# Attention over all tokens: the products with the values in a budget per turn, and none of them in a block's extra turn

## The chip, the core and the metric

One NeuronCore of a Trainium2 chip runs the whole kernel in one launch. TensorE (PE in the profile) multiplies matrices, ScalarE (ACT) evaluates functions, VectorE (DVE) adds and divides, GpSimd (POOL) does some adds and issues DMAs, SyncE (SP) issues DMAs. The metric is the device time of one execution in microseconds (us), the median of three runs. Lower is better.

## The reference, cut to what matters

The model is a chain of four layers on 4 images of 56 x 56 positions with 128 channels. The first layer attends within windows, and then over all 3136 positions of an image; the second part is what the change touches. Everything is float32.

```python
def _mha(x, wq, bq, wk, bk, wv, bv, wo, bo):
    n, s, c = x.shape                      # s = 3136, c = 128, NH = 4 heads, dk = 32
    q = (x @ wq + bq).reshape(n, s, NH, dk).transpose(0, 2, 1, 3)
    ...
    scores = jnp.einsum('nhqd,nhkd->nhqk', q, k) / jnp.sqrt(jnp.float32(dk))
    attn = jax.nn.softmax(scores, axis=-1)
    out = jnp.einsum('nhqk,nhkd->nhqd', attn, v)
    out = out.transpose(0, 2, 1, 3).reshape(n, s, c)
    return out @ wo + bo
...
xf = x.reshape(B, H * W, C)
xf = xf + _mha(_layernorm(xf, g1, be1), wq, bq, wk, bk, wv, bv, wo, bo)
h = jax.nn.gelu(_layernorm(xf, g2, be2) @ w1 + b1, approximate=False)
xf = xf + (h @ w2 + b2)
```

After this layer come a graph layer over pairs of positions in a row, a Fourier layer with its own attention over rows, and a convolution. They are not changed.

## The kernel before, in words

The kernel works through the four images one after the other: `fast_attention` (which first calls `fast_windows` for the attention in windows and for the queries, keys and values), then the multilayer perceptron, then the graph layer. When all four are done, the Fourier layer, its attention and the last convolution follow. Each of these stages needs the result of the one before, so the attention loop of an image stands on the way to everything after it.

`fast_attention` cuts the 3136 queries of an image into 7 blocks of 448 (`NBLK`, `NB`). For each block it goes through the keys in 24 chunks of 128 and a remainder of 64, which it counts as chunk 24. A chunk of a block has four tiles, one for each head: 128 keys by 448 queries of scores. So a block has 96 tiles and an image 672. They are counted through, over the ends of blocks.

The loop takes 7 tiles per *turn* (`TURN`), so an image has 96 turns. A turn has two halves, of four tiles and of three:

- PE multiplies the queries and keys (L698) into a PSUM tile, `s0` of four banks for the first half and `s1` of three for the second. Each has one buffer.
- ACT takes the exponential of all tiles of the half in one instruction (L701) and writes it into a ring in SBUF of 28 tiles (`RING`), which is 7 chunks or four turns. A tile's slot is its number modulo 28.
- For every chunk that is now complete, `add` issues the sum over the keys, which is the denominator of the softmax: DVE adds the chunk to a running sum (L626, L630); chunks 1, 5, 9, 13 and 17 (`BY_DMA`) are instead copied (SP, L618) or added (POOL, L620) into a second sum by DMA, which DVE adds in (L629) ahead of the block's last chunk. In the last block chunks 21 to 23 are left to a product with ones on PE.

Then `values` issues the products of the exponentials with the values (L642). A chunk is four products of 32 columns each, one per head, side by side in the array, summed in one PSUM bank (`f_po`). The lists `queue` and `ready` give them a lag of one turn: a turn's `values` takes all chunks in `ready`, up to the end of a block, and then moves the chunks that this turn completed from `queue` to `ready`. As 7 tiles are 1.75 chunks, the turns have 2, 2, 2 and 1 chunks in rotation. When chunk 23 is through, ACT copies the block's sum out of the bank (L645).

Two turns after a block's tiles began to be complete for the block before (`AFTER`, `ends`), an *extra turn* follows the ordinary one. It has three parts:

- `remainder(j)`: the scores of the 64 last keys of the block j that has begun (L660, into `s0`), and their exponential (L663, tile `f_p`);
- `values` once more, with whatever is ready;
- `finish(j - 1)`: the denominators of the block before, as products with ones: of DVE's sum (L671) and of the remainder (L674), into `s1`; then the output product of the block before that one (L677); a copy by ACT (L679), the reciprocal (L680) and the product (L681) by DVE, and the addition to the residual (L686).

The order of PE, ACT and DVE in this loop is the order of the program: it is written out by hand (`manual_schedule`), and each engine works through its own list in that order. PE writes into `s0` or `s1` only when ACT has read what was in it, and ACT writes into a slot of the ring only when PE, DVE or the DMA have read it.

One float32 matmul stands in the trace as two, its two passes through the array. So a first half of scores is x8 in the timeline, a whole turn of scores x14, and a chunk of values x8. The matmul columns read rows * columns of the array, then the shape that streams.

Of the kernel before, what the change touches and what calls it, by code (L numbers as in the profile page):

```python
# [23 lines left out]
NB = 448  # L24
# [16 lines left out]
def blk(j):  # L41
    return slice(j * NB, (j + 1) * NB)
# [524 lines left out]

RING = 28
TURN = 7
BY_DMA = (1, 5, 9, 13, 17)  # L570
BY_ONES = ()
LAST_ONES = (21, 22, 23)
# [3 lines left out]
def fast_attention(k, w, xw, xf, beside, mr):  # L576

    nc, tc = k.nc, k.tc
    scale = 1.0 / math.sqrt(32.0)
    heads = [slice(32 * h, 32 * h + 32) for h in range(4)]
    half = (slice(0, 64), slice(64, 128))
    with ExitStack() as es:
        big = es.enter_context(tc.tile_pool(name="f_big", bufs=1))
        qT = big.tile([P, TOK], F32, name="f_qT")
        kT = big.tile([P, TOK], F32, name="f_kT")
        va = big.tile([P, 25, P], F32, name="f_va")  # L590
        fast_windows(k, w, xw, xf, mr, beside, qT, kT, va)

        ring = es.enter_context(tc.tile_pool(name="f_ring", bufs=1)).tile([P, RING, NB], F32, name="f_ring")
        wk = es.enter_context(tc.tile_pool(name="f_wk", bufs=2))
        ps = es.enter_context(tc.tile_pool(name="f_ps", bufs=1, space=PSUM))
        oT = es.enter_context(tc.tile_pool(name="f_out", bufs=1)).tile([P, TOK], F32, name="f_oT")
        blocks = [Env() for _ in range(NBLK)]
        queue, ready = [], []

        def by_ones(j):  # L600
            return LAST_ONES if j == NBLK - 1 else BY_ONES

        def bank(turn):
            return ps.tile([P, (4, 3)[turn], 512], F32, tag="s%d" % turn, name="f_s%d" % turn)

        def slots(j, c):
            s = (96 * j + 4 * c) % RING
            return ring[:, s:s + 4, :]

        def add(j, c):  # L610

            e = blocks[j]
            if c in by_ones(j):
                return
            if c in BY_DMA:
                if c == BY_DMA[0]:
                    e.far = wk.tile([P, 4, NB], F32, name="f_far", bufs=1)
                    nc.sync.dma_start(e.far, slots(j, c))  # L618
                else:
                    nc.gpsimd.dma_start(e.far, slots(j, c), accum_op=ALU.add)  # L620
                return
            if c == 0:
                return
            if not hasattr(e, "acc"):
                e.acc = wk.tile([P, 4, NB], F32, name="f_acc")
                nc.vector.tensor_add(e.acc, slots(j, 0), slots(j, c))  # L626
                return
            if BY_DMA and c == last_add(j):
                nc.vector.tensor_add(e.acc, e.acc, e.far)  # L629
            nc.vector.tensor_add(e.acc, e.acc, slots(j, c))  # L630

        def last_add(j):
            return max(c for c in range(24) if c not in BY_DMA and c not in by_ones(j))

        def value(j, c):
            e = blocks[j]
            if c == 0:
                e.po = ps.tile([P, 512], F32, tag="po", name="f_po")
            for h in range(4):
                o = half[h % 2] if c == 24 else slice(0, P)  # L640
                p = e.p24[o, h // 2, :] if c == 24 else slots(j, c)[:, h, :]
                nc.tensor.matmul(e.po[heads[h], :NB], va[o, c, heads[h]], p, start=(c == 0), stop=(c == 23))  # L642
            if c == 23:
                e.raw = wk.tile([P, NB], F32, name="f_raw")
                nc.scalar.copy(e.raw, e.po[:, :NB])  # L645

        def values():

            while ready:
                j, c = ready.pop(0)  # L650
                value(j, c)
                if c == 23:
                    break
            ready.extend(queue)
            queue.clear()

        def remainder(j):
            ss = bank(0)
            for h in range(4):
                nc.tensor.matmul(ss[half[h % 2], h // 2, :NB], kT[heads[h], 24 * P:TOK], qT[heads[h], blk(j)],  # L660
                                 start=True, stop=True)
            blocks[j].p24 = wk.tile([P, 2, NB], F32, name="f_p24")
            nc.scalar.activation(blocks[j].p24, ss[:, 0:2, :NB], AF.Exp, scale=scale)  # L663

        def finish(j):

            e = blocks[j]
            pd = bank(1)
            for n, p in enumerate([e.acc] + [slots(j, c) for c in by_ones(j)]):
                for h in range(4):  # L670
                    nc.tensor.matmul(pd[heads[h], 0, :NB], k.ones[:, 0:32], p[:, h, :], start=(n == 0), stop=False)  # L671
            for h in range(4):
                o = half[h % 2]
                nc.tensor.matmul(pd[heads[h], 0, :NB], k.ones[o, 0:32], e.p24[o, h // 2, :], start=False, stop=True)  # L674
            m = 1 + (j > 0)
            if j:
                nc.tensor.matmul(pd[:, 1, :NB], w.wo, oT[:, blk(j - 1)], start=True, stop=True)  # L677
            den = wk.tile([P, 2, NB], F32, name="f_den")
            nc.scalar.copy(den[:, :m], pd[:, :m, :NB])  # L679
            nc.vector.reciprocal(den[:, 0], den[:, 0])  # L680
            nc.vector.tensor_mul(oT[:, blk(j)], e.raw, den[:, 0])  # L681
            if j:
                output(j - 1, den[:, 1])

        def output(j, pm):
            nc.vector.scalar_tensor_tensor(xf[:, blk(j)], pm, w.fbvo, xf[:, blk(j)], ALU.add, ALU.add)  # L686

        with tc.manual_schedule(engines={mybir.EngineType.PE, mybir.EngineType.Activation, mybir.EngineType.DVE}):
            t = 0
            ends = {-(-96 * j // TURN) - 1 + AFTER: j for j in range(NBLK)}  # L690
            for turn in range(96 * NBLK // TURN):
                for half_turn in range(2):
                    m = (4, 3)[half_turn]
                    ss = bank(half_turn)
                    for i in range(m):
                        j, c = divmod((t + i) // 4, 24)
                        h = (t + i) % 4
                        nc.tensor.matmul(ss[:, i, :NB], kT[heads[h], c * P:(c + 1) * P], qT[heads[h], blk(j)],  # L698
                                         start=True, stop=True)
                    slot = t % RING  # L700
                    nc.scalar.activation(ring[:, slot:slot + m, :], ss[:, :m, :NB], AF.Exp, scale=scale)  # L701
                    for q in range(t // 4, (t + m) // 4):
                        queue.append(divmod(q, 24))
                        add(*divmod(q, 24))
                    t += m
                values()
                if turn in ends:
                    j = ends[turn]
                    remainder(j)
                    values()  # L710
                    if j:
                        finish(j - 1)
                    queue.append((j, 24))
            while ready or queue:
                values()
            finish(NBLK - 1)
        pm = ps.tile([P, 512], F32, tag="po", name="f_pf")
        nc.tensor.matmul(pm[:, :NB], w.wo, oT[:, blk(NBLK - 1)], start=True, stop=True)
        output(NBLK - 1, pm[:, :NB])
# [1750 lines left out]
def build(k, packs, I, out):  # L2470
# [3 lines left out]
    with ExitStack() as es:  # L2474
# [15 lines left out]
        with tc.tile_pool(name="w01", bufs=1) as wp, tc.tile_pool(name="io", bufs=1) as io:  # L2490
# [47 lines left out]
            with tc.If(small_scores > 0) as small:  # L2538
                for b in range(B):
                    first_layers(lambda *a: fast_attention(*a, functools.partial(norms, b - 1), k.mr[:, b, :]), I["x"][b],  # L2540
                                 x2d[b] if b < B - 1 else None, loaded=b == 0)
# [78 lines left out]
```

## Time and profile before

| | us |
|---|---|
| median of 3 runs | 3779.57 |
| lowest and highest | 3778.22, 3781.8 |
| the profiled execution, its own time | 3777.02 |
| the profiled execution, its span | 3775.2 |
| busy in the span: PE, DVE, ACT, POOL | 3456.1, 2762.1, 2069.6, 1305.6 |
| the four attention loops in the trace | 151.6 to 515.0, 847.5 to 1210.2, 1544.0 to 1906.7, 2239.7 to 2606.7 |

The span is from the first instruction to the last on the core; 1.8 us of the profiled execution's time lie around it. In a line of groups stand the line, engine, operation, output and inputs, shapes and count, then the busy time in us and the mean of one in ns, then the idle time before these instructions and what ended it. In a timeline stand the start and length in us of instructions of one kind that follow each other, and in brackets the idle time before them and what ended it. The length of a matmul includes its way through the array, which lies beside the next one, so the cost of a group in a stream is read from start to start. Some matmul records can be missing, so a count in the timeline may be short.

### The profile page before, as it was taken

The numbers are of one execution on the slowest core, as the hardware profiler recorded it, in microseconds if no ns is written. First come the engines' busy times: TensorE is split into PE (matmuls) and PEld (weight loads), VectorE is DVE, ScalarE is ACT, GpSimd is POOL, SyncE is SP. The second block draws the span as 40 slices with busy tenths as digits, with TensorE's granted clock in tenths as the row PEclk, the third lists the DMA queues.
The fourth block names the chain that finished last, engine by engine and source line by source line (L and its number), as shares of the span: only waits on it lengthen the run. The fifth ranks groups of instructions, "written<-read, shape, count | busy, mean of one in ns | idle before, by whom it ended". The sixth has DMA issues, their size and how long they took to land. (4 is left out here: it accounts for less than half of the span.)

```text
span 3775.2 us, 78990 instructions
## 1 busy us (share of the span) xinstructions
PE 3456.1 (92%) x35064; PEld 1544.1 (41%) x35064; DVE 2762.1 (73%) x2635; ACT 2069.6 (55%) x2052; POOL 1305.6 (35%) x779
## 2 busy tenths in 40 slices
PE   6899999989999998899989989999997889998998
PEld 4422234552223455322244542223456433335664
DVE  6488877857887786688869748887785767775676
ACT  4587865448777554687745448876553001213452
POOL 0000016600000471000018400000663769993676
PEclk8999999999999998999999999999998999999999
DMA  2134310004333000244310013443002047862011
GB/s 98 39 87 91 89 40 19 20 18 98 86 90 70 19 3 19 76 89 97 88 30 3 19 37 89 98 89 83 2 9 86 2 84 154 171 139 86 30 40 52
DMA packets 93656, 239.56 MB, mean 63 GB/s; under 512 B 64380, under 2 KB 66172, under 8 KB 88060
## 3 DMA queue, kind: packets, MB, share of 16 engines
q0 software_dynamic: 16128, 102.77, 13.6%
q1 hardware_dynamic: 18492, 118.82, 9.9%
q10 hardware_dynamic: 58688, 12.85, 2.0%
q8 instruction: 277, 4.54, 0.5%
q14 instruction: 71, 0.58, 0.1%
HBM read 79.46 MB, written 26.51 MB: 28 GB/s over the span
## 5 line engine op out<-in xcount | busy, mean ns | idle before, releaser
L701 ACT ACTIVATE f_ring<-f_s 128x1792 f32<-128x1792 f32 (+1 forms) x768 | 1091.5, 1477 | 186.1 <-PE f_s L698 125.4
L630 DVE TENSOR_TENSOR f_acc<-f_acc,f_ring 128x1792 f32<-128x1792 f32 x464 | 939.5, 2025 | 174.0 <-ACT f_ring L701 142.1
L698 PE MATMUL f_s<-f_qT,f_kT 32*128 32x448 f32 x5376 | 723.0, 573 | 66.3 <-ACT f_ring L701 42.5
L620 POOL DMA_DIRECT2D f_far<-f_ring x112 | 96.4, 861 | 1693.5 <-ACT f_ring L701 1441.7
L642 PE MATMUL f_po<-f_ring,f_va 128*32 128x448 f32 x5376 | 584.8, 546 | 0.0
L1063 DVE TENSOR_TENSOR e_td<-e_pa,e_c 128x1792 f32<-128x1792 f32 x252 | 491.2, 2012 | 14.4 <-ACT e_a L1028 14.4
L1065 POOL TENSOR_TENSOR e_tp<-e_a,e_c 128x1792 f32<-128x1792 f32 x140 | 451.9, 3258 | 143.8 <-PE e_acc L1070 104.8
L698 PEld LDWEIGHTS f_s<-f_qT,f_kT 32*128 32x128 f32 x5376 | 256.7, 183 | 537.5 <-ACT f_ring L701 410.7
L1070 PE MATMUL e_acc<-e_td,t_shared 32*32 32x448 f32 x8064 | 322.9, 545 | 21.8 <-DVE e_td L1063 10.6
L1067 ACT ACTIVATE e_tp<-e_tp 128x1792 f32<-128x1792 f32 x140 | 235.1, 1697 | 174.3 <-POOL e_tp L1065 174.3
L1679 DVE TENSOR_TENSOR u_ud<-u_px,u_d 112x1792 f32<-112x1792 f32 x144 | 240.1, 1707 | 94.8 <-PE u_po L1684 85.7
L642 PEld LDWEIGHTS f_po<-f_ring,f_va 128*32 128x32 f32 x5376 | 135.8, 109 | 396.3 <-issue 383.3
L1070 PE MATMUL e_acc<-e_tp,t_shared 32*32 32x448 f32 x4480 | 221.2, 544 | 3.2 <-ACT e_tp L1067 2.5
L1684 PE MATMUL u_po<-u_ud,AT 112*64 112x448 f32 x960 | 200.7, 548 | 23.3 <-DVE u_ud L1679 23.3
L1681 POOL TENSOR_TENSOR u_up<-xh,u_d 112x1792 f32<-112x1792 f32 x64 | 193.8, 3054 | 24.0 <-PE u_po L1684 12.4
L1070 PEld LDWEIGHTS e_acc<-e_td,t_shared 32*32 32x32 f32 x8064 | 133.3, 103 | 147.1 <-DVE e_td L1063 55.8
L680 DVE RECIPROCAL f_den<-f_den 128x448 f32<-128x448 f32 x28 | 82.7, 2953 | 94.7 <-ACT f_den L679 94.7
L1546 POOL TENSOR_TENSOR q_u<-iS,q_g 128x1792 f32<-128x1792 f32 x32 | 102.8, 3236 | 72.1 <-PE s_px L1394 48.0
L1684 PE MATMUL u_po<-u_up,AT 112*64 112x448 f32 x576 | 125.1, 541 | 0.9 <-POOL u_up L1681 0.8
L1684 PEld LDWEIGHTS u_po<-u_ud,AT 112*64 112x64 f32 x960 | 64.8, 137 | 147.6 <-issue 86.6
L1070 PEld LDWEIGHTS e_acc<-e_tp,t_shared 32*32 32x32 f32 x4480 | 94.5, 103 | 55.6 <-ACT e_tp L1067 19.1
L891 ACT ACTIVATE m_hT<-m_ph,w_fb 128x392 f32<-128x392 f32 x128 | 72.7, 588 | 70.4 <-PE m_ph L890 64.9
(487 smaller groups left out, 4746.0 us busy)
## 6 DMA issues: line engine op xcount, KB each, us to landing
f_far<-f_ring POOLq DMA_DIRECT2D x112, 896.0 KB, 6.4
u_d<-dd SPq DMA_DIRECT2D x48, 784.0 KB
f_far<-f_ring SPq DMA_DIRECT2D x28, 896.0 KB
xw<-in_x SPq DMA_DIRECT2D x4, 1568.0 KB
x2d<-x SPq DMA_DIRECT2D x4, 1568.0 KB
xad<-x SPq DMA_DIRECT2D x4, 1568.0 KB
x_xs<-xad ACTq DMA_DIRECT2D x32, 196.0 KB
xm<-x_ev ACTq DMA_DIRECT2D x64, 98.0 KB
```

The lines of the kernel that those rows point to most:

```text
L630: nc.vector.tensor_add(e.acc, e.acc, slots(j, c))
L642: nc.tensor.matmul(e.po[heads[h], :NB], va[o, c, heads[h]], p, start=(c == 0), stop=(c == 23))
L698: nc.tensor.matmul(ss[:, i, :NB], kT[heads[h], c * P:(c + 1) * P], qT[heads[h], blk(j)], start=True, stop=True)
L701: nc.scalar.activation(ring[:, slot:slot + m, :], ss[:, :m, :NB], AF.Exp, scale=scale)
L1063: nc.vector.tensor_tensor(t, am, cm, ALU.max)
L1065: nc.gpsimd.tensor_sub(t, bc(a.rearrange("p (l n) -> p l n", l=8), 1, 4), cm)
L1067: nc.scalar.activation(tf, tf, AF.Relu)
L1070: nc.tensor.matmul(acc[quarters[q], r, :NB], k.ident[o, o], t[o, q].rearrange("p l n -> p (l n)"), start=(g == 0), stop=(g == len(EDGE_TUR ...
L1546: nc.gpsimd.tensor_mul(u, bc(st.iS[:, bp, c, :HH], 1, HEADS), bc(g[:, n, c, :], 2, HH))
L1679: nc.vector.tensor_mul(u, bc(px[:, :, :NB], 2, m), dm)
L1681: nc.gpsimd.tensor_mul(u, bc(x, 2, m), dm)
L1684: nc.tensor.matmul(po[64 * b2:64 * b2 + 64, :NB], st.AT[:, 8 * i + h0 + q, 2 * bp + b2, :], u[:, b2, q, :], start=(left == 16), stop=(left ...
```

## The change

Four things are changed in `fast_attention`:

- A chunk's products with the values can be split into two halves of 224 queries. An entry of `ready` now has a part: the whole (`WHOLE`) or one half.
- `values` takes a budget of half chunks, `ROOM`: 3, 3, 4 and 4 in turns 0, 1, 2 and 3 of every four, and one more where more than three entries are waiting. Where one half of room is left, it does half of a chunk and leaves the other half first in the list. It still ends at chunk 23. What is left stays in `ready`.
- In the extra turn there is no `values`. The remainder's own product with the values (chunk 24) is done at the end of `finish` if the block has begun its products, and is else put into the list. Before, it was queued.
- In `finish` the output product of the earlier block stands ahead of the product of ones with the remainder, and not behind it.

After the last turn the list is emptied with a budget of 4 a call. In the order of issue an image has 52 halves, two for each of 26 split chunks. The lists of DVE, POOL and SP keep their order; in ACT's, four of the seven copies of L645 stand one turn later.

```diff
+ROOM = (3, 3, 4, 4)
+WHOLE = slice(0, NB)
...
-        def value(j, c):
+        def value(j, c, part):
             e = blocks[j]
-            if c == 0:
+            if c == 0 and part.start == 0:
                 e.po = ps.tile([P, 512], F32, tag="po", name="f_po")
             for h in range(4):
                 o = half[h % 2] if c == 24 else slice(0, P)
-                p = e.p24[o, h // 2, :] if c == 24 else slots(j, c)[:, h, :]
-                nc.tensor.matmul(e.po[heads[h], :NB], va[o, c, heads[h]], p, start=(c == 0), stop=(c == 23))
-            if c == 23:
+                p = e.p24[o, h // 2, part] if c == 24 else slots(j, c)[:, h, part]
+                nc.tensor.matmul(e.po[heads[h], part], va[o, c, heads[h]], p, start=(c == 0), stop=(c == 23 and part.stop == NB))
+            if c == 23 and part.stop == NB:
                 e.raw = wk.tile([P, NB], F32, name="f_raw")
                 nc.scalar.copy(e.raw, e.po[:, :NB])
-
-        def values():
-
-            while ready:
-                j, c = ready.pop(0)
-                value(j, c)
-                if c == 23:
+                return True
+
+        def values(room):
+
+            while ready and room > 0:
+                j, c, part = ready.pop(0)
+                if room == 1 and part == WHOLE:
+                    part = slice(0, NB // 2)
+                    ready.insert(0, (j, c, slice(NB // 2, NB)))
+                room -= 2 if part == WHOLE else 1
+                if value(j, c, part):
                     break
-            ready.extend(queue)
-            queue.clear()
...
-        def finish(j):
+        def finish(j, left=None):
...
+            m = 1 + (j > 0)
+            if j:
+                nc.tensor.matmul(pd[:, 1, :NB], w.wo, oT[:, blk(j - 1)], start=True, stop=True)
             for h in range(4):
                 o = half[h % 2]
                 nc.tensor.matmul(pd[heads[h], 0, :NB], k.ones[o, 0:32], e.p24[o, h // 2, :], start=False, stop=True)
-            m = 1 + (j > 0)
-            if j:
-                nc.tensor.matmul(pd[:, 1, :NB], w.wo, oT[:, blk(j - 1)], start=True, stop=True)
+            if left is not None:
+                value(left, 24, WHOLE)
...
-                        queue.append(divmod(q, 24))
+                        queue.append((*divmod(q, 24), WHOLE))
                         add(*divmod(q, 24))
                     t += m
-                values()
+                values(ROOM[turn % 4] + (len(ready) > 3))
+                ready.extend(queue)
+                queue.clear()
                 if turn in ends:
                     j = ends[turn]
                     remainder(j)
-                    values()
-                    if j:
-                        finish(j - 1)
-                    queue.append((j, 24))
-            while ready or queue:
-                values()
+                    if not j:
+                        ready.append((0, 24, WHOLE))
+                    else:
+                        started = hasattr(blocks[j], "po")
+                        finish(j - 1, j if started else None)
+                        if not started:
+                            ready.append((j, 24, WHOLE))
+            while ready:
+                values(4)
             finish(NBLK - 1)
```

## The prediction

> **What bounds the kernel now.** I read the share of the engines first, then the costliest groups of the page, then the timeline inside the loop that the diff edits. The groups:
>
> ```profile
> L701 ACT ACTIVATE f_ring<-f_s 128x1792 f32<-128x1792 f32 (+1 forms) x768 | 1091.5, 1477 | 186.1 <-PE f_s L698 125.4
> L630 DVE TENSOR_TENSOR f_acc<-f_acc,f_ring 128x1792 f32<-128x1792 f32 x464 | 939.5, 2025 | 174.0 <-ACT f_ring L701 142.1
> L698 PE MATMUL f_s<-f_qT,f_kT 32*128 32x448 f32 x5376 | 723.0, 573 | 66.3 <-ACT f_ring L701 42.5
> L642 PE MATMUL f_po<-f_ring,f_va 128*32 128x448 f32 x5376 | 584.8, 546 | 0.0
> ```
>
> Scores (L698), exponentials (L701), sums (L630) and value products (L642) are the four dearest groups of the edited code. They lie in one loop, run once for each of 4 samples. Busy time of the engines in the first sample's loop, from its first score to the end of its last denominators:
>
> ```profile
> 151.60:515.00 363.40, 347.36 (x2948) 106.31 (x2948) 286.98 (x147) 289.65 (x215) 24.22 (x28) 1.00 0.40 90
> ```
>
> Columns after the length: PE, PE loads, DVE, ACT, POOL, clock. PE is the fullest (347 of 363 us), but a busy PE counts the tails of matmuls, so the waits have to be found in the timeline. Four ordinary turns of the loop:
>
> ```profile
> 226.52 1.78 PE L698 MATMUL f_s<-f_qT,f_kT 32*128 32x448 f32 x14
> 228.23 1.71 PE L642 MATMUL f_po<-f_ring,f_va 128*32 128x448 f32 x16
> 229.87 1.78 PE L698 MATMUL f_s<-f_qT,f_kT 32*128 32x448 f32 x14
> 231.58 0.96 PE L642 MATMUL f_po<-f_ring,f_va 128*32 128x448 f32 x8
> 232.69 1.03 PE L698 MATMUL f_s<-f_qT,f_kT 32*128 32x448 f32 x8
> 233.87 1.03 PE L698 MATMUL f_s<-f_qT,f_kT 32*128 32x448 f32 x6
> 234.83 1.71 PE L642 MATMUL f_po<-f_ring,f_va 128*32 128x448 f32 x16
> 236.47 1.78 PE L698 MATMUL f_s<-f_qT,f_kT 32*128 32x448 f32 x14
> ```
>
> and ACT in the same turns:
>
> ```profile
> 227.62 2.85 ACT L701 ACTIVATE f_ring<-f_s 128x1792 f32<-128x1792 f32 x2 [0.51 <-PE f_s L698]
> 230.97 5.66 ACT L701 ACTIVATE f_ring<-f_s 128x1792 f32<-128x1792 f32 x4 [0.51 <-PE f_s L698]
> 237.57 2.85 ACT L701 ACTIVATE f_ring<-f_s 128x1792 f32<-128x1792 f32 x2 [0.94 <-PE f_s L698]
> ```
>
> Starts give the prices. The seven scores of a turn take 228.23 - 226.52 = 1.71 us. Two chunks of values (x16: 2 chunks, 4 heads, two passes each) take 229.87 - 228.23 = 1.64. One chunk alone, where nothing waits, takes 0.89 (322.65 to 323.54 below is such a one), so a chunk is 0.75 and a change of the array's tiling about 0.14. A turn with two chunks is 3.35 us and PE sets it; ACT works 2.85 and idles 0.5. A turn with one chunk would be 1.71 + 0.89 = 2.60, less than ACT's 2.85. Then ACT sets it: the two turns from 229.87 to 236.47 take 6.60 against 2.60 + 3.35 = 5.95 of PE work, and PE has lost 0.65. Nothing gives it back, for PE sets the next turns. A block's extra turn, to the second turn after it:
>
> ```profile
> 312.56 0.98 PE L660 MATMUL f_s<-f_qT,f_kT 32*64 32x448 f32 x8
> 313.47 1.71 PE L642 MATMUL f_po<-f_ring,f_va 128*32 128x448 f32 x16
> 315.00 0.94 PE L671 MATMUL f_s<-f_acc,c_ones 128*32 128x448 f32 x8
> 315.86 0.96 PE L674 MATMUL f_s<-f_p,c_ones 64*32 64x448 f32 x8
> 316.75 1.02 PE L677 MATMUL f_s<-f_oT,t_first 128*128 128x448 f32 x2
> 317.70 2.09 PE L698 MATMUL f_s<-f_qT,f_kT 32*128 32x448 f32 x14
> 320.51 2.21 PE L698 MATMUL f_s<-f_qT,f_kT 32*128 32x448 f32 x14 [0.72 <-ACT f_ring L701]
> 322.65 0.96 PE L642 MATMUL f_po<-f_p,f_va 64*32 64x448 f32 x8
> 323.54 0.96 PE L642 MATMUL f_po<-f_ring,f_va 128*32 128x448 f32 x8
> ```
>
> The extra turn takes two chunks that PE has no need to do there; ACT, which gets no scores, stands still. Then the turn at 317.70 has no values at all: 2.81 us to 320.51 for 1.71 of work, and the next takes 3.92 (to 324.43) for 3.48. PE loses 1.10 + 0.44 = 1.54.
>
> **What the Trainium skill says.** "TensorE: Matmul & The Clock Gate", section "Step-by-step: what each phase is for", has weights of later matmuls loaded while earlier ones run; the trace agrees (a group of four loads takes 0.13 us inside a pass of 0.37). Its section "Wait — 56ns, not 53.3ns?" gives a floor of about 25 ns from start to start for a small matmul, so four of a half pass would need 0.10 us; an estimate, and the trace's own row below is used instead. "TensorEngine Tiling (Array Packing)", section "Key Properties", says that a change of tiling mode drains TensorE; that is the 0.14 above, and halves do not change the mode.
>
> **The change, part by part.** PE's own work in one sample's loop before: 96 turns x 1.71 = 164.2; 175 chunks (168 and 7 remainders) x 0.747 = 130.7; 96 groups of values x 0.15 for the switch back and its gap = 14.4; 7 remainders x (0.91 + 0.14) = 7.4; 7 finishes x (0.87 + 0.87) + 6 output products x 0.95 + three more chunks of ones in the last block x 0.75 = 20.1. Sum 336.8. The loop takes 363.4, so PE waits 26.6. The order of issue has 22 turns with one chunk and 6 with none after the extra turns: 22 x 0.65 + 6 x 1.54 = 23.5, and the rest is the start (ACT's table load). So the waits are explained, and they are what the change can win.
>
> *Budget of 3 and 4 half chunks.* Seven chunks per four turns as before, so nothing is left over. A turn of three halves costs 1.71 + 3 x 0.373 + 0.15 + 0.02 = 3.00, one of four 3.35. ACT's second exponential of a turn ends 1.10 + 2.85 = 3.95 after the turn's start; the next turn's second group of scores needs its bank and could start at 3.00 + 0.75 = 3.75, so it waits until about 4.02: 0.27 lost. After the second turn of three halves ACT ends at 6.8, and the second group comes at 7.0: no wait. So four turns take 2 x 3.00 + 2 x 3.35 + 0.27 = 12.97, where they took 239.82 - 226.52 = 13.30. At most 24 such pairs stand in a sample, about 20 undisturbed by block ends: 20 x 0.27 = 5.4 of waits remain.
>
> *A half is a new operation*: 224 columns, 52 of them in a sample. Streaming at this trace's rate (448 columns per 0.373 us pass) it takes 0.187 a pass. Nearest row: the score products of the windows (L381, 196 columns, two tiles beside each other), 16 in 1.38 us, 0.172 per pair against 0.163 at that rate: 0.01 over. I take 0.02 per half (two passes): 1.0 us per sample. Lower bound 0, as columns must stream. Upper bound: the loads do not hide, 0.13 per pass, 0.26 per half, 13.5 us, of which the 0.27 wait of the pairs would swallow some 5.4: net 8 us less gain per sample.
>
> *No chunk in the extra turn.* The two chunks move to the two turns behind it, which then have 3 or 4 halves and wait as ordinary turns do. The 1.54 goes; what comes is a wait in the finish: it starts 0.91 after L660 and needs the bank of the second exponential, which ends 3.95 after the turn before began. Behind a four-half turn (3.35 + 0.91) it waits for nothing, behind a three-half one or one that stops at chunk 23 for 0.1 to 0.9. I take 0.5 for each of 6: 3.0. DVE's last sum before it ended at 309.38, 361.05 and 411.66 for blocks that start the extra turn at 312.56, 361.08 and 412.84, so the new start, 0.91 after L660, has 0.94 us to spare in the tightest and 4.1 in the widest. In two of the six the chunk of the remainder lands behind the ones (PE 0.75, ACT's copy runs beside it); in four the block has not begun and it is queued: the same work. Moving the output product ahead of the remainder's ones changes no work and covers the remainder's exponential (0.91 + 0.87 + 0.95 = 2.7 us against 1.05 + 0.92).
>
> *The ring.* Chunks now lag by up to five in the queue. An exponential overwrites a slot four turns later; in the order of issue every chunk read from such a slot stands before that turn's scores, so PE gives no new wait. The order of DVE's and POOL's instructions is unchanged: a loop that is 14 us shorter leaves DVE 287 busy of 350, and chunks for the accumulating DMA come every 7.4 instead of 7.6 us, with 0.86 to issue and 6.4 to land: 7.3, just under. *The end*: three chunks instead of two stay for the drain, contained in the work.
>
> Sum for one sample: work 336.8 + 1.0 + 0.2 (one more group) = 338.0; waits 5.4 + 3.0 + 3.1 for the start = 11.5; together 349.5 to 349.8, against 363.4: 13.8 less. Four samples run alike (loops of 363.4, 362.7, 362.7 and 367.0 us) and what follows each waits for it: 4 x 13.8 = 55 us. The profiled execution took 3777.0 (span 3775.2), which would be 3722; the median is 2.6 above it, so 3724.5.
>
> **Rivals.** *Dear halves*: loads or issue bind a half pass. For it: no row has this shape. Against: L381, and 66-column matmuls (L396) at 0.065 a pair. With 0.26 per half the gain is 13.8 + 1.0 - 8 = some 6.5 per sample: 3754. *Nothing gained*: a half pass costs a whole one, 52 x 0.373 = 19.4 a sample less what the pairs swallow: within 6 us of 3779. *Slower*: DVE is late at the block's end. Place: L671 now starts 1.5 us sooner after L660, on the path of PE and of the copy on ACT behind it. It decides once the last sum ends over 0.9 us after L660 begins; each us beyond costs 24 us in the kernel (6 blocks, 4 samples). With some 2.3 us to spare on the mean of the three blocks above, sums that end 6 us later against L660 than now lose 3.7 a block: 24 x 3.7 = 89, less 55: 3813. For it: DVE would be 287 of 350 busy, and one block is tight. Against: DVE still waits for L701 142 us in all ahead of its sums, so it is not behind.
>
> **Chances.** Forecast 0.78 (3714 to 3738: 2 us per sample for the waits that I took by hand, and halves at 0 to 0.07); dear halves 0.13 (to 3754); nothing gained 0.04; slower 0.05. The range takes in the dear halves: 3714 to 3754. About 0.2% (7.6 us) is what a measurement of this kernel tells from no change: faster 0.90, same 0.05, slower 0.05.
>
> **What would show it.** Turns of 3.0 and 3.35 us, pairs of three halves with a wait of 0.27 and nowhere 2.82 and 3.78; 224-column passes 0.19 us apart; the extra turn at 4.4 us and no turn without values; loops of 350 us. Wrong if the passes of halves stand 0.3 apart, if L671 waits for f_acc, or if L701 waits for DVE, PE's values or a DMA.

## The result and the profile after

| | us | ratio to before |
|---|---|---|
| before, median of 4 runs on the same chip | 3778.89 (3775.48 to 3781.8) | |
| changed, median of 4 runs | 3725.82 (3721.67 to 3730.92) | 0.9861 (0.9843 to 0.9878) |
| forecast | 3724.5 (3714 to 3754) | |
| profiled execution, its own time and span | 3726.18 and 3724.4 | |

The changed kernel is 53 us faster. The groups of the page that answer to the four shown of before (line, engine, operation, tiles and shapes, count, busy us and mean ns of one, then idle time ahead):

```profile
L707 ACT ACTIVATE f_ring<-f_s 128x1792 f32<-128x1792 f32 (+1 forms) x768 | 1092.9, 1475 | 175.4 <-PE f_s L704 128.1
L632 DVE TENSOR_TENSOR f_acc<-f_acc,f_ring 128x1792 f32<-128x1792 f32 x464 | 939.6, 2025 | 159.7 <-ACT f_ring L707 129.1
L704 PE MATMUL f_s<-f_qT,f_kT 32*128 32x448 f32 x5376 | 710.9, 570 | 19.6 <-ACT f_ring L707 9.8
L644 PE MATMUL f_po<-f_ring,f_va 128*32 128x448 f32 (+1 forms) x6176 | 585.2, 497 | 0.0
```

The busy times of ACT, DVE and the values have hardly moved. What moved is the idle time of PE ahead of the scores, from 66.3 to 19.6 us, and the busy time of the scores themselves, from 723.0 to 710.9: a wait inside a group of scores counts as busy, as where seven scores are 2.21 us long in the prediction's lines and not 1.78. Together that is 58.8 us less, of which the extra turns give some back (below). 800 more matmuls of whole chunks and half chunks with the values (6176 for 5376) cost 0.4 us of busy time. The first image's loop, same columns as before (length, PE, PE loads, DVE, ACT, POOL, clock):

```profile
151.94:501.80 349.86, 344.14 (x3156) 112.12 (x3156) 286.91 (x147) 290.14 (x215) 24.29 (x28) 1.00 0.42 93
```

13.5 us shorter than 363.40. Four ordinary turns on PE, budget 3, 3, 4, 4 half chunks ("halves" from here on):

```profile
181.03 1.78 PE L704 MATMUL f_s<-f_qT,f_kT 32*128 32x448 f32 x14
182.74 1.34 PE L644 MATMUL f_po<-f_ring,f_va 128*32 128x448 f32 x16
184.00 2.05 PE L704 MATMUL f_s<-f_qT,f_kT 32*128 32x448 f32 x14
185.98 1.34 PE L644 MATMUL f_po<-f_ring,f_va 128*32 128x224 f32 x16
187.25 1.83 PE L704 MATMUL f_s<-f_qT,f_kT 32*128 32x448 f32 x14
189.01 1.71 PE L644 MATMUL f_po<-f_ring,f_va 128*32 128x448 f32 x16
190.65 1.78 PE L704 MATMUL f_s<-f_qT,f_kT 32*128 32x448 f32 x14
192.36 1.71 PE L644 MATMUL f_po<-f_ring,f_va 128*32 128x448 f32 x16
194.00 0.66 PE L704 MATMUL f_s<-f_qT,f_kT 32*128 32x448 f32 x4
```

and on ACT in the same turns:

```profile
182.13 2.85 ACT L707 ACTIVATE f_ring<-f_s 128x1792 f32<-128x1792 f32 x2 [0.51 <-PE f_s L704]
185.15 2.85 ACT L707 ACTIVATE f_ring<-f_s 128x1792 f32<-128x1792 f32 x2 [0.18 <-ACT f_ring L707]
188.35 2.85 ACT L707 ACTIVATE f_ring<-f_s 128x1792 f32<-128x1792 f32 x2 [0.35 <-PE f_s L704]
```

The turns take 2.97, 3.25, 3.40 and 3.35 us: 194.00 - 181.03 = 12.97, where it was 13.30. A turn of three halves that waits for nothing is 1.71 + 1.26. The remaining wait is read in the second: its scores take 185.98 - 184.00 = 1.98 for 1.71, because the second group waits for ACT to have read its bank. ACT waits a little in each of these turns (the brackets) and does not run through two of them at its own pace, as it did for 5.66 us before. It still does so elsewhere: from 325.50 it runs through two turns in 5.66 us. The extra turn of the same block as shown of before:

```profile
306.75 0.98 PE L664 MATMUL f_s<-f_qT,f_kT 32*64 32x448 f32 x8
...
311.14 1.78 PE L704 MATMUL f_s<-f_qT,f_kT 32*128 32x448 f32 x14
312.85 1.34 PE L644 MATMUL f_po<-f_ring,f_va 128*32 128x448 f32 x16
```

It takes 311.14 - 306.75 = 4.39 us, with the ones, the output product and the remainder's values in between, and the turn behind it has three halves (312.85) and is not empty. At another block the wait that the prediction set for the finish is seen, behind a turn that stopped early at chunk 23:

```profile
255.34 0.98 PE L664 MATMUL f_s<-f_qT,f_kT 32*64 32x448 f32 x8 [0.25 <-ACT f_ring L707]
256.52 0.96 PE L675 MATMUL f_s<-f_acc,c_ones 128*32 128x448 f32 x8 [0.20 <-ACT f_ring L707]
```

Both waits are for ACT, none for DVE's sum. In all four images L664 idles 2.9 us and L675 3.6, 3.2 of them for ACT and none for DVE; together that is 6.5 us, where the same two groups idled 0.0 and 0.8 us before. The four loops now take 349.9, 349.6, 349.6 and 351.1 us, 1400.2 together, 55.6 less than the 1455.8 of before. The profiled span fell by 50.8, as the rest of the kernel took 4.8 us longer in this execution; single runs of the changed kernel lie 9 us apart. The loops repeat far better than that: those of a second trace of the changed kernel (after_again) take 1400.1 us together.

### The profile page after: what moved, and what is told of

Its sections match the earlier page's. It is cut to its first block, busy times and chain, and to the rows that moved or that the text cites. A ratio compares the mean times of both kernels' runs of the same rounds, so it can differ in the third digit from the quotient of the medians.

```text
span 3724.4 us, 80654 instructions
## 1 busy us (share of the span) xinstructions
PE 3447.2 (93%) x35896; PEld 1571.6 (42%) x35896; DVE 2758.1 (74%) x2635; ACT 2071.4 (56%) x2052; POOL 1306.0 (35%) x779
## 3 DMA queue, kind: packets, MB, share of 16 engines
q0 software_dynamic: 16128, 102.77, 13.8%
## 5 line engine op out<-in xcount | busy, mean ns | idle before, releaser
L707 ACT ACTIVATE f_ring<-f_s 128x1792 f32<-128x1792 f32 (+1 forms) x768 | 1092.9, 1475 | 175.4 <-PE f_s L704 128.1
L704 PE MATMUL f_s<-f_qT,f_kT 32*128 32x448 f32 x5376 | 710.9, 570 | 19.6 <-ACT f_ring L707 9.8
L644 PE MATMUL f_po<-f_ring,f_va 128*32 128x448 f32 (+1 forms) x6176 | 585.2, 497 | 0.0
L644 PEld LDWEIGHTS f_po<-f_ring,f_va 128*32 128x32 f32 x6176 | 161.3, 109 | 405.0 <-issue 390.4
L1692 POOL TENSOR_TENSOR u_up<-xh,u_d 112x1792 f32<-112x1792 f32 x64 | 193.8, 3055 | 24.0 <-PE u_po L1695 12.4
L1081 PEld LDWEIGHTS e_acc<-e_tp,t_shared 32*32 32x32 f32 x4480 | 94.8, 103 | 55.6 <-ACT e_tp L1078 19.5
L1779 ACT COPY x_ev<-x_po 56x896 f32<-56x896 f32 x32 | 28.8, 901 | 151.2 <-DMA xm<-x_ev 76.6
```

The costliest lines, as they stand in the source:

```text
L644: nc.tensor.matmul(e.po[heads[h], part], va[o, c, heads[h]], p, start=(c == 0), stop=(c == 23 and part.stop == NB))
L1081: nc.tensor.matmul(acc[quarters[q], r, :NB], k.ident[o, o], t[o, q].rearrange("p l n -> p (l n)"), start=(g == 0), stop=(g == len(EDGE_TUR ...
L1692: nc.gpsimd.tensor_mul(u, bc(x, 2, m), dm)
```

## Experiments

The theory: what was won is PE's waiting for ACT, in turns with too few products and in empty turns. A turn with no values is called empty, and the list has a stock when more waits in `ready` than the turn takes. The rivals: a half is dear and eats part of the gain; evenness alone counts, whatever stands next to what; or the two parts of the change win apart from each other, as the prediction's steps booked them. In the table, the values of a turn are given in halves, counted in the order of issue for one image (96 turns); the loops are the four of the kept trace, from the first score to the end of the last denominators.

| kernel | turns with 4 or more halves | 3 | 1 or 2 | 0 | four loops, us | median us | ratio to before on its chip |
|---|---|---|---|---|---|---|---|
| before | 66 | 0 | 22 | 8 | 1456 | 3778.89 | 1 |
| whole_no_extra | 72 | 0 | 23 | 1 | 1421 | 3744.22 | 0.9900 (0.9885 to 0.9916) |
| extra_kept | 43 | 43 | 9 | 1 | 1408 | 3732.65 | 0.9878 (0.9863 to 0.9893) |
| changed | 52 | 38 | 5 | 1 | 1400 | 3725.82 | 0.9861 (0.9843 to 0.9878) |

**whole_no_extra**: the second part alone, no values in the extra turn.

```diff
             while ready and room > 0:
                 j, c, part = ready.pop(0)
-                if room == 1 and part == WHOLE:
-                    part = slice(0, NB // 2)
-                    ready.insert(0, (j, c, slice(NB // 2, NB)))
...
-                values(ROOM[turn % 4] + (len(ready) > 3))
+                values(4)
```

> The second part of the change alone: chunks are never split, a turn takes up to two whole chunks, and the extra turn takes none. Theory (waits of PE are what was won): the chunks that the extra turn leaves keep a stock in the list, so the turns behind it take two chunks and none is empty; only when the stock is used up do turns with one chunk come back, with 0.65 us lost at each. Worked through turn by turn with the starts of the trace of before this gives 10 us less per image: about 3739. Rival (the halves do the work and the extra turn only moves chunks about): within 10 us of before, about 3770 or more.

Measured: 3744.22 against 3780.94 on its chip, 36.7 us faster, 9.2 per image. PE's list behind the extra turn (first scores of the next turn at 313.88):

```profile
313.88 1.78 PE L701 MATMUL f_s<-f_qT,f_kT 32*128 32x448 f32 x14
...
330.63 2.00 PE L701 MATMUL f_s<-f_qT,f_kT 32*128 32x448 f32 x14
...
337.23 1.78 PE L701 MATMUL f_s<-f_qT,f_kT 32*128 32x448 f32 x14
```

Five turns of two chunks, 3.35 us each, follow the extra turn (330.63 - 313.88 = 5 x 3.35); then the stock is used up and the pair of turns with one and two chunks is back: 330.63 to 337.23 is 6.60 us. The rival, that the extra turn only moves chunks about, falls. There are as many turns with one chunk as before (23 for 22), so what is won is the empty turns: six at 1.54 us are 9.2 per image.

**extra_kept**: the first part alone, the budget.

```diff
                     remainder(j)
+                    values(4)
                     if not j:
                         ready.append((0, 24, WHOLE))
                     else:
-                        started = hasattr(blocks[j], "po")
-                        finish(j - 1, j if started else None)
-                        if not started:
-                            ready.append((j, 24, WHOLE))
+                        finish(j - 1)
+                        ready.append((j, 24, WHOLE))
```

> The first part of the change alone: the budget of 3, 3, 4, 4 half chunks, but the extra turn takes up to two chunks as before. Theory: the turns with one chunk go, an empty or near empty turn behind the extra turn stays; worked through turn by turn 12 us less per image, about 3730, so the two parts overlap and do not add up. Rival (the parts add up, 55 us in all): what this one wins and what the other part alone wins make 53 us together.

Measured: 3732.65, 48.3 us faster. The parts alone win 36.7 and 48.3, together 85, and both at once 53: they overlap. (The place of the output product is new in both runs, but cannot be what is counted twice: before, PE idled 0.0 us ahead of L674 and of L677.) On top of the budget the second part is worth little: the intervals of extra_kept and the changed kernel overlap, and in the traces the loops differ by 8 us. PE behind the extra turn, which here takes two chunks:

```profile
311.27 2.12 PE L704 MATMUL f_s<-f_qT,f_kT 32*128 32x448 f32 x14
313.32 0.96 PE L644 MATMUL f_po<-f_ring,f_va 128*32 128x448 f32 x8
```

The turn at 311.27 is not empty although the extra turn took its two chunks: the budget had left a stock. So the empty turns of before had two causes that were both needed, the extra turn's taking and a list without stock, and either part of the change removes them (the one that is left in the table is an image's first turn, which has nothing to take).

**halves_before_order** and **quarters_before_order**: the price of a part by itself, in the order of before.

```diff
-            for h in range(4):
...
+            n = NB // 2 if 0 < c < 24 else NB
+            for i in range(0, NB, n):
+                for h in range(4):
...
+                    nc.tensor.matmul(e.po[heads[h], i:i + n], va[o, c, heads[h]], p, start=(c == 0), stop=(c == 23 and i + n == NB))
```

(with `NB // 4` for quarters.)

> The kernel before with its own order, but each of the chunks 1 to 23 issued as two halves of 224 columns, one right behind the other: the price of a half by itself. If a half pass costs its columns (0.187 us): within 4 us of before. At 0.02 us per half as the prediction took it: 322 halves x 4 images x 0.02 = 26 us slower, less what lies in turns with one chunk: 3800. If loads do not hide (0.26 per half): over 4000.

> As the halves in the order of before, but each of the chunks 1 to 23 is issued as four quarters of 112 columns. If a pass costs its columns (0.093 us) at any width: within 5 us of before. If the four loads and four matmuls of a pass have a floor like the 66-column matmuls of the windows (0.065 us a pair, so 0.13 for four): 0.037 x 2 passes x 644 quarters x 4 images = 190 us slower, about 3960. If loads of 0.13 us stand beside every pass: more than 1000 us slower.

Measured: halves 3780.80 against 3780.94, ratio 1.0002 (0.9993 to 1.001): nothing that can be told. Quarters 3791.02, ratio 1.0029 (1.002 to 1.0039): 10 us slower. PE of the halves, two chunks and the next scores:

```profile
229.13 1.72 PE L644 MATMUL f_po<-f_ring,f_va 128*32 128x224 f32 x32
230.78 1.78 PE L700 MATMUL f_s<-f_qT,f_kT 32*128 32x448 f32 x14
```

Two chunks take 1.64 us whole, 1.65 as halves (230.78 - 229.13), and 1.67 as quarters (226.59 to 228.26 in their timeline): four times as many matmuls add 0.03 us, 2.5 ns for each of 12 more passes (a pass is the four heads beside each other). The whole kernel agrees: 10 us over 3864 more passes is 2.6 ns. Dear halves fall, and so do the 0.02 us per half of the prediction.

**order_3434** and **order_3444**: only the order or the sum of the budget, here the first (the second has `(3, 4, 4, 4)`).

```diff
-ROOM = (3, 3, 4, 4)
+ROOM = (3, 4, 3, 4)
```

> The changed kernel with its budget in the order 3, 4, 3, 4: the same work, only the two turns of three halves no longer stand together. Theory: each turn of three halves that follows one of four makes the next turn's second group of scores wait 0.3 us for ACT; together only the first of a pair does, apart both do. Four turns then take 2 x 3.00 + 2 x 3.35 + 2 x 0.3 = 13.3 in place of 12.97; worked through turn by turn, where the stock of chunks plays in, some 5 us more per image: about 3747. Rival (only evenness of the values counts): as the changed kernel, 3726.

Measured: 3753.13, ratio 0.9932 (0.9919 to 0.9945), where the changed kernel has 0.9861: 27 us given back with the same columns to stream and nearly the same mix of turns (51 of four or more, 39 of three). It splits 48 chunks in place of 26, which by halves_before_order costs nothing that can be told. PE:

```profile
225.50 1.78 PE L704 MATMUL f_s<-f_qT,f_kT 32*128 32x448 f32 x14
...
228.47 2.05 PE L704 MATMUL f_s<-f_qT,f_kT 32*128 32x448 f32 x14
230.45 1.72 PE L644 MATMUL f_po<-f_ring,f_va 128*32 128x224 f32 x24
...
235.08 2.05 PE L704 MATMUL f_s<-f_qT,f_kT 32*128 32x448 f32 x14
237.06 1.71 PE L644 MATMUL f_po<-f_ring,f_va 128*32 128x448 f32 x16
238.70 1.78 PE L704 MATMUL f_s<-f_qT,f_kT 32*128 32x448 f32 x14
```

The scores behind each turn of three halves take 1.98 (228.47 to 230.45, 235.08 to 237.06); four turns take 13.20 against 12.97. Side by side, the scores behind the first of two take 1.98 and those behind the second 1.76 (184.00 and 187.25 above), for PE has been held up by then. That confirms the 0.27 of the prediction, and that neighbours count, not evenness alone. 0.23 us in four turns makes some 22 of the 27 us; the rest was not followed up.

> The changed kernel with a budget of 3, 4, 4, 4: one half more than comes in, so only one turn of three in four while there is stock, and the list is shorter. Theory: fewer turns of three with their wait, but the list runs dry sooner: 1 us less per image, about 3722, at the edge of what can be told from the changed kernel. Rival (the list has to stay stocked): slower than the changed kernel by 10 us or more.

Measured: 3717.81, ratio 0.9834 (0.9821 to 0.9847); the list needs no larger stock. The reason expected does not hold, though: in the order of issue this kernel has 38 turns of three, as many as the changed one. What differs is that no turn has five halves (nine have in the changed kernel), and that three or four halves stand ahead of each of the six extra turns with a finish, where the changed kernel has one or two ahead of four of them. L664 and L675 idle 1.0 us together here and 6.5 in the changed kernel, the scores 22.4 and 19.6, so the ends of the blocks are the likely place of a gain; no run changes them alone. Side by side on one chip, with the changed kernel:

> The changed kernel itself, beside the budget of 3, 4, 4, 4 on one chip, to see which of the two is faster. Expected: 0.986 of before, as measured.

> The budget of 3, 4, 4, 4 beside the changed kernel on one chip. Theory: about 1 us less per image, so 4 to 8 us faster than the changed kernel (0.984 of before). Rival (the gain seen was the chip's spread): equal to the changed kernel.

Measured: 3727.10, ratio 0.9861 (0.9842 to 0.9881), and 3723.99, ratio 0.9851 (0.9834 to 0.9867). Both times 3, 4, 4, 4 is ahead, by 8 and by 3 us, but the intervals overlap, so the run times leave open whether it beats the changed kernel. The traces tell more: its four loops take 1395.4 and 1395.6 us in two traces, those of the changed kernel 1400.2 and 1400.1. That is 4.7 us, 1.2 per image, about what was expected, and too little for the run times to show.

**more_sums_on_dve**: the slower rival of the prediction, made to happen.

```diff
-BY_DMA = (1, 5, 9, 13, 17)
+BY_DMA = (1, 5)
```

> The changed kernel with three of the five chunks per block taken from the accumulating DMA and given to DVE (BY_DMA of 1 and 5), so DVE has 3 x 2.08 = 6.2 us more per block. This tests the slower rival of the prediction, that DVE is late at the block's end and the finish waits for its sum. If DVE's slack is what the timeline says (1 to 4 us ahead of the finish at the ends of blocks, and caught up within a block): waits of 0 to 2 us at the ends of blocks, 5 us per image: about 3747. If DVE is already the bound: 6.2 x 28 = 174 us slower, 3900. If it has slack for all: 3726.

Measured: 3797.98, ratio 1.0052 (1.004 to 1.0064), some 72 us slower than the changed kernel, over three times what I expected. The wait stands where the rival put it (groups, idle time ahead last):

```profile
L675 PE MATMUL f_s<-f_acc,c_ones 128*32 128x448 f32 x224 | 32.1, 646 | 54.2 <-DVE f_acc L632 54.2
L681 PE MATMUL f_s<-f_p,c_ones 64*32 64x448 f32 x224 | 35.5, 712 | 0.0
```

54.2 us over 28 blocks is 1.9 us each, so some 4.3 of the 6.2 us more per block were taken up by slack. The sum was late at 24 of the 28 blocks, so DVE had less room than I had assumed. The wait is not all of the 72 us: it explains 50.6, for L675 idled 3.6 in the changed kernel. Behind the wait the matmuls of the finish also ran longer (L681 has a mean of 712 ns, 548 in the changed kernel); the busy times of its four groups of matmuls rose by 22.5 us, which makes 73 with the wait. The granted clock (1.00 is TensorE's full speed) was low there: 0.55 from 909.5 to 913 us, right behind a wait of 2.71 us, and 1.00 in the 3 us after. By this run, as an estimate, the changed kernel is about 4 us per block away from such waits on the mean, and about 2 at an image's fourth block, where the wait was 3.9 to 4.4 us.

**no_values**: the loop without the products of chunks 1 to 22.

```diff
-            for h in range(4):
+            for h in range(4 if c in (0, 23, 24) else 0):
```

> The changed kernel without the products of chunks 1 to 22 with the values (the output leaves their part out): what bounds the loop when PE does not. Theory: ACT paces the turns at 2.85 us and DVE (287 us busy per image) holds the ring now and then, some 318 us per image against 350: about 3598. So the work of PE that remains costs 32 us per image at most, and no order of the values could win more than the waits of about 12 us per image that are left. Rival (PE's waits, not its work, still set the time): above 3680.

Measured: 3628.80, 0.9594 (0.9582 to 0.9607): 97 us below the changed kernel, where I expected 128. The rival falls: PE's products with the values still set 97 us of the time. The size was off. L675 waited 28.0 us for DVE and L707 12.4 us for a DMA, and the mean granted clock of TensorE was lower, 0.952 in place of 0.967; how the missing 31 us divide between them is not shown. Nor does this run tell what the waits that are left would give, as it takes work and waits away together.

## Why the prediction was right

- *PE waits are what can be won.* Shown: the idle time of PE ahead of the scores fell from 66.3 to 19.6 us, the work stayed, and four loops fell by 55.6 us where 55 were worked out. The median fell by 53.1.
- *Four turns in 12.97 us.* Measured 12.97. The 0.27 that one of two short turns loses was predicted from ACT's pace and is confirmed by order_3434, where the scores behind both lose it.
- *A half at 0.02 us.* Too high: nothing measurable for 322 halves per image. The upper bound of 0.26 was far off. (The sum for the dear halves, 13.8 + 1.0 - 8, is 6.8 and not 6.5, which puts that end of the range near 3752; nothing rests on it.)
- *The extra turn.* Predicted 4.4 us, measured 4.39. The waits for ACT at the finish were booked at 3.0 us per image; L664 and L675 idle 1.6.
- *The sum.* It came out closer than its terms, and that is partly luck. In the first image's loop the scores behind the start are held up by 7.0 us in all, where 5.4 was booked; the finish and the halves cost about 1.4 and 1.0 us less than booked. The errors nearly cancel: 349.9 us for 349.5 to 349.8.
- *Which part wins what.* The steps booked 6 x 1.54 less 3.0 = 6.2 us per image (25 us) on the extra turn, and the rest, some 30 us, on the budget; alone they win 37 and 48. The second part wins its 6 x 1.54 in full, as the 3.0 at the finish do not come (L661 and L672 of its own trace idle 0.0 and 0.9 us in all). The budget wins more than its share because the stock it leaves in the list also fills the empty turns, which the prediction had put down to the extra turn alone.
- *DVE's slack.* The slower rival did not come, as argued, but the reason given (it still waits for ACT, so it is not behind) was too easy: with 6.2 us more per block PE waited 1.9 us for it on the mean. The rival's price, 24 us for each us at 24 blocks, also left out that the matmuls behind such a wait run at a lower clock.
- *The rest of the kernel.* 4.8 us longer in the profiled execution. 3.5 of them lie between the third and the fourth loop, where PE was busy 303.4 us and 299.4 before, at a mean granted clock of 0.94 and 0.96; the second trace of the changed kernel has the same length there (336.4 us, before 333.0). Why the clock was lower stays open.

## What to carry to other kernels

Where two engines take turns on single buffers, as here, a turn lasts about as long as the slower of the two in it, so work that could move between turns should be spread until one engine is the slower in all of them; the sum of busy times does not show the loss, the starts of turns do. A lagged list of work did better here with a small stock and a budget than with "all that is ready", and with short turns side by side. Test each part of such a change alone: their gains need not add up. And where a change is too small for the run times, compare the stage itself in two traces of each kernel, if it repeats as well as these loops did.

## What the runs showed of the hardware

- Splitting a float32 product of four 128 x 32 tiles from 448 to 224 and to 112 streamed columns cost 2.5 ns per additional pass, with the loads of every pass included. The Trainium skill, "TensorE: Matmul & The Clock Gate", section "The mechanism", lists that loads overlap with matmuls in flight only where the row groups differ, while its text also lets a load into the background weight buffer go ahead. Here all four tiles use the same 128 rows, and the loads cost nothing that could be measured at 224 columns, so the "only" does not hold for this shape; the measurement decides.
- Behind long waits of PE the granted clock was low for a few us, so such a wait cost more than its length. In more_sums_on_dve it was 0.97 from 906 to 909.5 us, where PE worked for 0.88 us and then waited for DVE, 0.55 from 909.5 to 913, and 1.00 from 913 to 916. Eight matmuls of L675 took 1.72 us there and 0.96 behind a wait of 0.93 us (at 260.98). How long a wait has to be was not measured. The mean clocks fit this (0.952 in the kernel without most value products, 0.960 where PE waited for DVE, 0.967 in the changed kernel), but for the mean no run separates this from other causes.
